# Where the first rows of x, the row moments and the diagonal sums are computed in a four-layer graph kernel, and in which order its second layer is entered

## The chip, the cores and the metric

The kernel runs on one core of a Trainium2 chip. The core has five engines with a queue each: TensorE (PE in the profile, its weight loads PEld), VectorE (DVE), ScalarE (ACT), GpSimd (POOL) and SyncE (SP), which here only issues DMA transfers. The engines run beside each other and wait for each other through semaphores; each queue is worked off in its order. The metric is the time of one execution on the device in microseconds (us), the median of several runs. Less is better.

## What is computed

Four graph layers over N = 2708 nodes with D = 128 features. Each has the form x = x + layer(relu(layernorm(x)), adj), with adj a 2708 x 2708 f32 matrix that is sparse but stored dense, and whose diagonal isn't zero. The reference, cut to the two layers that matter here:

```python
# layer 0
h = maximum(layernorm(x), 0)
msg = adj.T @ h
inv_deg = 1 / adj.sum(axis=0)             # 0 where infinite
x = x + msg * inv_deg[:, None]

# layer 1
h = maximum(layernorm(x), 0)
s = h @ msg_w[:, :D].T ;  d = h @ msg_w[:, D:].T
messages = gelu(s[:, None, :] + d[None, :, :] + msg_b)
agg = einsum('ijd,ij->id', messages, adj)
new = gelu(concat([h, agg]) @ upd_w.T + upd_b) + h
x = x + layernorm(new) * ln_w + ln_b
# layer 2: adj @ h and a GRU cell;  layer 3: two attention heads masked by adj
```

The kernel doesn't form all pairs in layer 1. For every row and every block of 124 columns, VectorE looks up the (at most 8) largest entries and their columns; this is done in layer 0, while adj passes through the memory on the chip. Layer 1 then works on those lists, with the diagonal taken apart.

## The kernel before

Rows go in tiles of 128 (22 tiles, NT), columns in blocks of 124 (22 blocks, NB). GROUPS are groups of four tiles (the last has two). At the start all of x is asked for on ScalarE's queue, and all 22 tiles are normalised ahead of layer 0. Cuts are marked (...).

```python
for t, k in GROUPS[:-1]:
    nc.scalar.dma_start(xs[:, t : t + k, :], x[t * P : (t + k) * P, :].rearrange("(t p) d -> p t d", p=P))
...                                            # two more loads for the last two tiles

def moments(src, name, pool=small):            # VectorE, and one power on GpSimd
    for q in range(k):
        nc.vector.bn_stats(st[:, q, :], src[q])
        nc.vector.bn_aggr(mv[:, q, :], st[:, q, :])
    nc.vector.tensor_scalar(r[:, 3, :], mv[:, :, 1], EPS, None, ALU.add)
    nc.gpsimd.tensor_tensor(r[:, 0, :], r[:, 3, :], minus_half[:, 0:k], ALU.pow)
    return mv, r
def factors(mv, r): ...                        # five small VectorE operations on [128, k]
def scale_rows(dst, src, rstd, shift, func):   # ScalarE, one activation a tile
    for q in range(len(src)):
        nc.scalar.activation(dst[q], src[q], func, bias=shift[:, q : q + 1], scale=rstd[:, q : q + 1])

for t, k in GROUPS:
    normalise(h, xs, t, k, AF.Relu, "n0")      # moments, factors, scale_rows
```

Layer 0. The tile rows of a group share one buffer `a4`, of which there are two. After the group, its 22 column tiles are turned on TensorE, and ScalarE takes them out with their sums and sends them to HBM for layers 2 and 3:

```python
for gi, (g0, gk) in enumerate(GROUPS):
    a4 = rows.tile([P, 4, N], F32, name="a")
    for q in range(gk):
        n = g0 + q
        a = a4[:, q, :]
        nc.sync.dma_start(a[0:m, :], adj[n * P : n * P + m, :])
        for ci, (c, cw) in enumerate(CHUNKS):  # six chunks of columns
            nc.tensor.matmul(accs[ci][:, 0:cw], h[0:m, n, :], a[0:m, c : c + cw], ...)
        nc.gpsimd.tensor_copy(near[:, 0 : c1 - c0], a[:, c0:c1])          # the blocks of the diagonal
        nc.gpsimd.tensor_tensor(dg[:, 0:m], a[:, d0 : d0 + m], ident[:, 0:m], ALU.mult)
        nc.gpsimd.tensor_tensor(near[:, ...], a[:, d0 : d0 + m], offdiag[:, 0:m], ALU.mult)
        nc.vector.reduce_sum(own[:, n : n + 1], dg[:, 0:m], AX.X)         # the diagonal, by row
        for b in range(NB):
            ...                                                           # ab: block b of a, or of near
            nc.vector.max(val[:, n, b, :], ab)
            nc.vector.max_index(col[:, n, b, :], val[:, n, b, :], ab)
        nc.scalar.activation(sign, a, AF.Sign, accum_out=total[:, n : n + 1])
    for j in range(NT):
        ...                                                               # transposes of the group
        nc.scalar.activation(aT[0:k, 0:iw], p[0:k, 0:iw], AF.Copy, accum_out=sums[0:k, j, gi : gi + 1])
        nc.sync.dma_start(adjT[0:k, j, i0 : i0 + iw], aT[0:k, 0:iw])
```

Layer 1 runs in periods, one for each tile t, and is pipelined over four tiles. A period works in six steps k; steps of later tiles are laid between the products of the present one:

```python
def period(t, between=()):
    now, c, b, a = (0 <= t + q < NT for q in range(4))
    last = 0 <= t - 1 < NT
    if c and not between:
        put_values(t + 1)                      # GpSimd, 8 operations
    for k in range(GB):
        for step in between[k : k + 1]:
            step()
        if now:
            combine(t, k)                      # TensorE, 24 products
            activate(t, k)
        if k < 2:
            if last: gather(t - 1, GB - 2 + k)
            if k == 0 and c: pass_on(t + 1)    # two DMAs, out to HBM and back, to all partitions
            if k == 1 and a: rank(t + 3)
            if k == 1 and last: close_tile(t - 1)
        elif now:
            gather(t, k - 2)
        if k in (1, 2) and b: fetch(t + 2, k - 1)
        if k == 1 and a: describe(t + 3)
        if k == 2:
            if now and t % 2 == 0 and t + 2 < NT: sources(t // 2 + 1)
            if a: select_rows(t + 3)           # VectorE: sel; then two DMAs: later = sel, one partition on
            if now and t + 4 < NT: count_rows(t + 4)
            updates(t)
        if k > 0 and c: put_more(t + 1, k)     # ScalarE, 14 in all
        if k == 3 and c: columns(t + 1)        # VectorE, on what pass_on brought
        if k == 3 and b: place(t + 2)          # VectorE, seven operations
        if k == 4 and a: finish_rows(t + 3)    # VectorE: sel -= later
```

Before the first period comes the prologue. For each group g of rows it adds layer 0's result to x (`enter`: scaled additions and moments on VectorE), scales (`rows`: factors on VectorE, scaling on ScalarE), turns (`turn_rows`: TensorE and ScalarE) and makes the columns' part of the messages (`destinations`: TensorE; its split into three bf16 parts goes ScalarE, VectorE, ScalarE, GpSimd). It also brings the first three tiles through rank, describe, select, finish, fetch and place. The kernel writes it as one list, in the order in which every engine gets its instructions:

```python
for step, n in (
    (spread_sums, 0), (count_rows, 0), (spread_sums, 1), (rank, 0), (enter, 0),
    (select_rows, 0), (describe, 0), (enter, 1), (spread_sums, 2), (rows, 0), (turn_rows, 0),
    (count_rows, 1), (rows, 1), (count_rows, 2), (count_rows, 3), (destinations, 0), (turn_rows, 1),
    (finish_rows, 0), (fetch_both, 0), (rank, 1), (enter, 2), ...
    (split_destinations, 3), (put_values, 0), (destinations, 4), (put_rest, 0), (finish_rows, 2),
):
    step(n)
period(0, (fourth, fifth))     # fourth, fifth: split of group 4, all of group 5, put_values(1)
for t in range(1, NT + 1):
    period(t)
```

Outside of such lists (`tc.manual_schedule`) the order of instructions on an engine is chosen when the kernel is built, so it isn't always that of the text.

Of the kernel before, what the change touches and what calls it, by code (L numbers as in the profile page):

```python
# [30 lines left out]
P = 128  # L31
N = 2708
# [28 lines left out]
def listed_layers(ctx: ExitStack, tc: tile.TileContext, x, adj, w, out, flag):  # L61
# [17 lines left out]
    for t, k in GROUPS[:-1]:  # L79
        nc.scalar.dma_start(xs[:, t : t + k, :], x[t * P : (t + k) * P, :].rearrange("(t p) d -> p t d", p=P))  # L80
    nc.scalar.dma_start(xs[:, FULL - 1, :], x[(FULL - 1) * P : FULL * P, :])
    nc.scalar.dma_start(xs[0:TAIL, FULL, :], x[FULL * P : N, :])
# [4 lines left out]
    def load(pool, name, shape=None):  # L87
        t = pool.tile(list(shape or w[name].shape), F32, name=name)
        nc.scalar.dma_start(t, w[name])
        return t  # L90

    def load_columns(pool, name):

        k = w[name].shape[0] // P
        t = pool.tile([P, k], F32, name=name)
        nc.scalar.dma_start(t, w[name].rearrange("(k p) -> p k", p=P), allow_slow_non_contiguous=True)
        return t

    def load_rows(pool, name):

        t = pool.tile([P, w[name].shape[0]], F32, name=name)
        nc.scalar.dma_start(t, w[name].partition_broadcast(P))
        return t


    minus_half = const.tile([P, 8], F32, name="minus_half")
# [50 lines left out]
    for t, k in GROUPS:  # L157
        normalise(h, xs, t, k, AF.Relu, "n0")
# [10 lines left out]
    HB = NB // 2  # L169
    HP = 8  # L170
    R = 4
    C = 4 * S + R + 1

    count = keep.tile([P, P], F32, name="count")
    nc.gpsimd.iota(count, [[1, P]], base=0, channel_multiplier=0, allow_small_or_imprecise_dtypes=True)
    count_h = keep.tile([P, P], BF16, name="count_h")
    nc.vector.tensor_copy(count_h, count)
    ident_h = keep.tile([P, P], BF16, name="ident_h")
    nc.vector.tensor_copy(ident_h, ident)
    part = keep.tile([P, 1], F32, name="part")  # L180
    nc.gpsimd.iota(part, [[0, 1]], base=0, channel_multiplier=1, allow_small_or_imprecise_dtypes=True)
    before = keep.tile([P, P], BF16, name="before")
    nc.vector.tensor_scalar(before, count, part, None, ALU.is_gt)
    ends4 = keep.tile([P, NB, R], BF16, name="ends4")
    rows_n = keep.tile([P, NT, NB], BF16, name="rows_n")
    ends = keep.tile([P, NT, NB], BF16, name="ends")
    later = keep.tile([P, NB, E], BF16, name="later")
    nc.gpsimd.memset(later, 0.0)
    xb = [keep.tile([P, NB, C], BF16, name=f"xb{q}") for q in range(2)]
    for q in range(2):  # L190
        nc.vector.tensor_copy(xb[q][:, :, 4 * S : 4 * S + R], part.unsqueeze(1).to_broadcast([P, NB, R]))

# [4 lines left out]
    with tc.tile_pool(name="l0c", bufs=1) as fix:  # L197
# [3 lines left out]
        nc.gpsimd.memset(sums, 1.0)  # L201
        with (
# [6 lines left out]
            for gi, (g0, gk) in enumerate(GROUPS):  # L209
# [4 lines left out]
                for q in range(gk):  # L214
# [3 lines left out]
                    nc.sync.dma_start(a[0:m, :], adj[n * P : n * P + m, :])  # L218
                    for ci, (c, cw) in enumerate(CHUNKS):
# [15 lines left out]
                    nc.vector.reduce_sum(own[:, n : n + 1], dg[:, 0:m], AX.X)  # L235
                    for b in range(NB):
# [4 lines left out]
                        nc.vector.max_index(col[:, n, b, :], val[:, n, b, :], ab)  # L241
                    sign = pool.tile([P, N], BF16, name="sign")
                    nc.scalar.activation(sign, a, AF.Sign, accum_out=total[:, n : n + 1])
                for j in range(NT):
# [31 lines left out]
    nc.vector.tensor_tensor(gate_b, b_ih[:, 0:2], b_hh[:, 0:2], ALU.add)  # L276
    nc.vector.tensor_scalar(gate_b, gate_b, 0.5, None, ALU.mult)
    half_b = late.tile([P, 1], F32, name="half_b")
    nc.vector.tensor_scalar(half_b, b_hh[:, 2:3], 0.5, None, ALU.mult)
# [6 lines left out]
    def layer3_weights():  # L286
# [13 lines left out]

    with (
# [18 lines left out]

        d3 = fix.tile([P, NB, 3, D], BF16, name="d3")
        def split(dst, src, rest):
# [273 lines left out]
        def period(t, between=()):  # L596
# [3 lines left out]
            if c and not between:  # L600
                put_values(t + 1)
            for k in range(GB):
                for step in between[k : k + 1]:
                    step()
# [36 lines left out]
        def spread_sums(g):  # L641
# [6 lines left out]
            state["p", g] = p  # L648

        def enter(g):  # L650

            t, k = GROUPS[g]
            p = state.pop(("p", g))
# [8 lines left out]
        def rows(g):  # L662
# [8 lines left out]
        def blocks_of(g):  # L671

            return 4 * g, min(4, NB - 4 * g)

        def destinations(g):

            b0, bn = blocks_of(g)
            p = bank("p_d")
            pv = p.rearrange("p (b d) -> p b d", b=4)
            for b in range(b0, b0 + bn):  # L680
                k = width(b)
                nc.tensor.matmul(pv[0:k, b - b0, :], hT[:, b * JB : b * JB + k], msg_wT[:, 1, :], start=True, stop=True)
            whole = bn if width(b0 + bn - 1) == JB else bn - 1
            state["d", g] = [
                (pv[0:k, q0:q1, :], [d3[0:k, b0 + q0 : b0 + q1, q, :] for q in range(3)], q0, q1, k)
                for q0, q1, k in ((0, whole, JB), (whole, bn, width(NB - 1)))
# [870 lines left out]
```

## Time and profile before

| what | value |
|---|---|
| time, median of 3 runs | 1110.0 us (1109.5 to 1110.35) |
| span of the profiled execution | 1108.1 us |
| TensorE busy, weight loads | 963.6 us (87%), 760.1 us (69%) |
| VectorE busy | 839.4 us (76%) |
| ScalarE busy | 504.2 us (46%) |
| GpSimd busy | 394.1 us (36%) |
| HBM read, written | 77.30 MB, 30.84 MB |
| mean granted clock of TensorE | 0.933 |

Busy times are sums over the whole span; the layers have different limits, so a stretch of the time has to be looked at by itself. A line of the timeline gives the start in us, the time of the instructions in us, the engine, the source line, the operation, what it writes and reads, how many were merged into the line, and in brackets how long the engine was idle before and what ended that. Times of instructions on one engine may overlap: a MAX8 lasts 0.28 us, and the next instruction starts 0.19 us after it. The source lines that matter: L116 to L119 are the moments, L125 to L129 the factors, L135 the scaling, L220 the products of layer 0, L235 the diagonal's sum, L240 and L241 the search, L243 the signs, L249 and L253 the transposes and their way out, L339 builds sel (and mine), L364 and L365 send later, L370 is finish_rows, L453 columns, L499 and L503 the products of layer 1.

### The profile page before, as it was taken

What the parts mean: (1) busy time and instruction counts of PE and PEld (TensorE: products, weight loads), DVE (VectorE), ACT (ScalarE), POOL (GpSimd) and SP (SyncE); (2) the same over time, 40 slices, a digit from 0 to 9 for tenths busy, and PEclk for the clock granted to TensorE, in tenths of its full rate; (3) what the DMA queues carried; (4) which work ended last, traced back from release to release, by engine and by line L of the source; (5) the groups of instructions that cost most, each with busy time, mean ns of one, the idle gap of its engine ahead of it and who ended that gap; (6) DMA issues with size and microseconds to landing.
All of it is one profiled execution on the core that took longest, in us unless ns stands there. A gap on an engine that the chain in (4) does not pass through costs nothing. (4 is left out here: it accounts for less than half of the span.)

```text
span 1108.1 us, 21904 instructions
## 1 busy us (share of the span) xinstructions
PE 963.6 (87%) x7968; PEld 760.1 (69%) x7968; DVE 839.4 (76%) x2948; ACT 504.2 (46%) x1319; POOL 394.1 (36%) x466
## 2 busy tenths in 40 slices
PE   3998887944389999999999979999979999999993
PEld 1455444523389999999898934444468899999772
DVE  5999999997766668676887255655578977997673
ACT  3857556623476666656676521433322200230142
POOL 4111111103385655776566253344310200340132
PEclk9999889755699999999999989999989999999996
DMA  9488978522133222322222056545300000000000
GB/s 361 164 299 281 324 259 288 178 64 68 46 106 102 96 86 90 106 86 101 83 103 80 28 193 209 190 157 198 100 18 1 1 9 1 1 20 1 2 15 14
DMA packets 55298, 125.39 MB, mean 113 GB/s; under 512 B 7414, under 2 KB 19782, under 8 KB 52472
## 3 DMA queue, kind: packets, MB, share of 16 engines
q1 hardware_dynamic: 48590, 121.12, 31.6%
q10 hardware_dynamic: 6590, 2.77, 1.0%
q8 instruction: 64, 1.05, 0.4%
q14 instruction: 54, 0.44, 0.1%
HBM read 77.30 MB, written 30.84 MB: 98 GB/s over the span
## 5 line engine op out<-in xcount | busy, mean ns | idle before, releaser
L838 PE MATMUL att<-hv,wt 128*128 128x129 f32 (+2 forms) x1936 | 240.7, 281 | 9.2 <-DVE wt L806 9.2
L838 PEld LDWEIGHTS att<-hv,wt 128*128 128x128 f32 (+2 forms) x1936 | 221.8, 190 | 26.2 <-DVE wt L806 9.1
L806 DVE SCALAR_TENSOR_TENSOR wt<-row,lift,mask 128x1024 f32<-128x1024 f32 (+5 forms) x176 | 160.0, 939 | 34.2 <-PE att L838 34.2
L423 POOL TENSOR_SCALAR put<-mine,value 128x128 f32<-128x128 bf16 x176 | 147.7, 855 | 72.4 <-DVE mine L339 70.0
L499 PE MATMUL p_m<-s,sel 128*128 128x128 bf16 x1452 | 160.8, 219 | 5.4 <-ACT g L511 5.4
L119 POOL TENSOR_TENSOR n_r<-n_r,minus_half 128x4 f32<-128x4 f32 (+1 forms) x36 | 51.3, 1425 | 316.1 <-DVE n_r L118 305.2
L503 PE MATMUL p_m<-d,cols 124*128 124x128 bf16 (+1 forms) x1452 | 161.0, 219 | 1.4 <-DVE cols L453 1.3
L220 PE MATMUL acc<-a,hs 128*128 128x512 f32 (+2 forms) x264 | 122.3, 599 | 27.6 <-DMA a<-in_adj 18.9
L524 PE MATMUL agg<-put,g 128*128 128x128 f32 (+1 forms) x968 | 135.8, 281 | 0.0
L241 DVE FIND_INDEX8 col<-val,a 128x8 uint16<-128x124 f32 (+1 forms) x441 | 118.6, 280 | 0.0
L959 PE MATMUL p_agg<-a,hs 128*128 128x512 f32 (+2 forms) x264 | 111.5, 564 | 7.7 <-DVE u L572 4.8
L524 PEld LDWEIGHTS agg<-put,g 128*128 128x128 f32 x968 | 118.1, 192 | 0.0
L499 PEld LDWEIGHTS <-sel 128*128 128x128 bf16 x1452 | 103.7, 97 | 10.8 <-issue 7.1
L503 PEld LDWEIGHTS <-cols 124*128 124x128 bf16 (+1 forms) x1452 | 101.8, 97 | 1.9 <-DVE cols L453 1.9
L240 DVE MAX8 val<-a 128x8 f32<-128x124 f32 (+1 forms) x441 | 102.6, 272 | 0.0
L511 ACT ACTIVATE g<-p_m 128x512 f32<-128x512 f32 x132 | 73.0, 553 | 63.6 <-PE p_m L503 63.6
L431 ACT ACTIVATE put<-mine,value 128x128 f32<-128x128 bf16 x308 | 100.5, 390 | 0.0
L220 PEld LDWEIGHTS acc<-a,hs 128*128 128x128 f32 (+1 forms) x264 | 49.7, 209 | 72.2 <-issue 43.4
L249 PEld LDWEIGHTS p_T<-ident,a 128*128 128x128 f32 x484 | 59.0, 146 | 52.8 <-ACT aT L253 25.4
L249 PE MATMUL p_T<-ident,a 128*128 128x128 f32 x484 | 77.7, 293 | 18.3 <-DMA a<-in_adj 10.0
L253 ACT ACTIVATE aT<-p_T 128x512 f32<-128x512 f32 (+2 forms) x132 | 70.9, 541 | 40.0 <-issue 16.3
L959 PEld LDWEIGHTS p_agg<-a,hs 128*128 128x128 f32 (+1 forms) x264 | 48.6, 196 | 56.6 <-issue 55.1
(228 smaller groups left out, 1396.6 us busy)
## 6 DMA issues: line engine op xcount, KB each, us to landing
a<-in_adj SPq DMA_DIRECT2D x21, 1354.0 KB
adjT<-aT SPq DMA_DIRECT2D x105, 256.0 KB
a<-adjT SPq DMA_DIRECT2D x20, 1280.0 KB
spread<-passed SPq DMA_DIRECT2D x22, 704.0 KB
later<-sel SPq DMA_DIRECT2D x22, 616.0 KB
later<-sel SPq DMA_DIRECT2D x22, 82.5 KB
adjT<-aT SPq DMA_DIRECT2D x21, 74.0 KB
a<-adjT SPq DMA_DIRECT2D x4, 370.0 KB
```

Of the source, the lines that this page charges most:

```text
L220: nc.tensor.matmul(accs[ci][:, 0:cw], h[0:m, n, :], a[0:m, c : c + cw], start=(n == 0), stop=(n == NT - 1))
L240: nc.vector.max(val[:, n, b, :], ab)
L241: nc.vector.max_index(col[:, n, b, :], val[:, n, b, :], ab)
L249: nc.tensor.transpose(p[0:k, q * P : q * P + m], a4[0:m, q, j * P : j * P + k], ident[0:m, 0:m])
L423: nc.gpsimd.tensor_scalar(st["put", 0][:, b, :], st["mine"][:, b, :], st["value"][:, b : b + 1], None, ALU.mult)
L431: nc.scalar.activation(st["put", 1][:, b - HP, :], st["mine"][:, b, :], AF.Identity, scale=st["value"][:, b : b + 1])
L499: nc.tensor.matmul(p[:, b - b0, :], st["sel"][:, b, :], s3[:, q, t % 2, :], start=(q == 0), stop=False)
L503: nc.tensor.matmul(p[:, b - b0, :], st["cols"][0:kb, b, :], d3[0:kb, b, q, :], start=False, stop=(q == 2))
L524: nc.tensor.matmul(agg, g[:, b - 4 * k, :], put, start=(b == 0), stop=False)
L806: nc.vector.scalar_tensor_tensor(wt[0:kj, :], row[0:kj, k, c : c + n], lift[0:kj, j, k : k + 1], mask[0:kj, j, c : c + n], op0=ALU.max, op ...
L838: nc.tensor.matmul(banks[s // 3][0:m, s % 3, :], wt[0:kj, q * P : q * P + m], hv[0:kj, j, k, :], start=(v < 2 and s // 3 not in touched), ...
L959: nc.tensor.matmul(pa[:, 0:n], h[0:k, j, :], a[0:k, j - j0, 0:n], start=(j == 0), stop=(j == NT - 1))
```

## The change

Two things at once.

Layer 0. The first four tiles of x are loaded ahead of adj on SyncE's queue, and only they are normalised ahead of layer 0; the rest of x follows behind the second tile row of adj. The moments of the other 18 tiles come from ScalarE, as sums and sums of squares of accumulating activations, with GpSimd for the small arithmetic; these are written behind the search of tile 2. The diagonal's sum goes from VectorE to ScalarE. Weights are loaded from SyncE's queue in place of ScalarE's. The purpose is to start the search earlier and to take work from VectorE in layer 0.

Prologue. The written list gives way to a loop over the groups, with periods -3, -2 and -1 put between; period 0 is like any other. The constants of layer 1 (count, part, before, later, xb) move from ahead of layer 0 into layer 1.

```diff
-    for t, k in GROUPS[:-1]:
-        nc.scalar.dma_start(xs[:, t : t + k, :], x[t * P : (t + k) * P, :].rearrange("(t p) d -> p t d", p=P))
-    ...
+    nc.sync.dma_start(xs[:, 0:4, :], x[0 : 4 * P, :].rearrange("(t p) d -> p t d", p=P))
+    def load_rest(): ...                    # the other rows, on nc.sync
 ...                                         # load, load_columns, load_rows: nc.scalar -> nc.sync
-    for t, k in GROUPS:
-        normalise(h, xs, t, k, AF.Relu, "n0")
+    normalise(h, xs, 0, 4, AF.Relu, "n0")
 ...                                         # count, part, before, later, xb: from here to layer 1
+        def moments_apart(pool):
+            for t in range(4, NT):
+                junk = pool.tile([P, D], F32, name="junk")
+                nc.scalar.activation(junk, xs[:, t, :], AF.Copy, accum_out=shifts[:, t - 4 : t - 3])
+            nc.gpsimd.tensor_scalar(shifts, shifts, -1.0 / D, None, ALU.mult)
+            for t in range(4, NT):
+                junk = pool.tile([P, D], F32, name="junk")
+                nc.scalar.activation(
+                    junk, xs[:, t, :], AF.Square, bias=shifts[:, t - 4 : t - 3], accum_out=ve[:, t - 4 : t - 3]
+                )
+            nc.gpsimd.tensor_scalar(ve, ve, 1.0 / D, EPS, ALU.mult, ALU.add)
+            nc.gpsimd.tensor_tensor(rstd, ve, minus_half[:, 0:RT], ALU.pow)
+            ...                              # five more of [128, 18] on nc.gpsimd
+            scale_rows(tiles_of(h, 4, RT), tiles_of(xs, 4, RT), rstd, shifts, AF.Relu)
                     nc.sync.dma_start(a[0:m, :], adj[n * P : n * P + m, :])
+                    if n == 1:
+                        load_rest()
-                    nc.vector.reduce_sum(own[:, n : n + 1], dg[:, 0:m], AX.X)
 ...                                         # the search
+                    if n == 2:
+                        moments_apart(pool)
                     nc.scalar.activation(sign, a, AF.Sign, accum_out=total[:, n : n + 1])
+                    nc.scalar.activation(dg[:, 0:m], dg[:, 0:m], AF.Copy, accum_out=own[:, n : n + 1])
 ...                                         # gate_b, half_b: computed in late_weights (layer 2)
-        def period(t, between=()):
+        def period(t):
-            if c and not between:
+            if c:
                 put_values(t + 1)
 ...
-            for step, n in ( ... the list ... ):
-                step(n)
-            period(0, (fourth, fifth))
-            for t in range(1, NT + 1):
+            for t in range(4):
+                count_rows(t)
+            steps = (enter, rows_and_turn, turn_rows, destinations)
+            fill = {0: -3, 2: -2, 4: -1}
+            for g in range(len(GROUPS) + len(steps) - 1):
+                for k in reversed(range(len(steps))):
+                    if 0 <= g - k < len(GROUPS):
+                        steps[k](g - k)
+                if g in fill:
+                    period(fill[g])
+            sources(0)
+            for t in range(NT + 1):
                 period(t)
```

In the new prologue `enter` holds spread_sums, `rows_and_turn` is the old rows, and `destinations` does its split at once.

## The prediction

> **What bounds the kernel now.** I read the 40 slices of the page first, then the busy times in stretches that I cut where the work changes, then the timeline at the three seams.
>
> The slices show who is full when; one slice is 27.7 us.
>
> ```profile
> PE   3998887944389999999999979999979999999993
> DVE  5999999997766668676887255655578977997673
> PEclk9999889755699999999999989999989999999996
> ```
>
> VectorE (DVE) is full from slice 2 to 9. Then TensorE and its clock sink for two or three slices, and after that TensorE is full to the end. So there are three regimes, and the change touches the first two. The stretches put times to them:
>
> ```profile
> core 0: us, PE busy (x) PEld busy (x) DVE busy (x) ACT busy (x) POOL busy (x), PEclk, DMA share, GB/s
> 0.00:21.40 21.40, 2.74 (x6) 1.42 (x7) 10.52 (x72) 5.77 (x8) 7.71 (x16) 1.00 0.97 341
> 21.40:244.20 222.80, 184.77 (x751) 106.89 (x750) 220.77 (x1493) 139.73 (x331) 31.56 (x67) 0.88 0.69 242
> 244.20:304.10 59.90, 23.79 (x133) 18.20 (x133) 47.28 (x159) 22.92 (x54) 16.71 (x20) 0.59 0.17 57
> 304.10:320.70 16.60, 13.64 (x194) 12.95 (x193) 9.14 (x17) 13.11 (x44) 15.87 (x22) 0.98 0.24 80
> 320.70:621.00 300.30, 291.34 (x4080) 281.27 (x4078) 220.23 (x422) 195.44 (x569) 190.34 (x239) 1.00 0.28 94
> ```
>
> In layer 0 (21.4 to 244.2) VectorE has 220.77 of 222.80 us, ScalarE 139.73, GpSimd 31.56. In the prologue of layer 1 (244.2 to 304.1) no engine is full; VectorE has the most, 47.28 of 59.90, so that stretch is a chain of waits. From 320.7 on the cycle is TensorE's.
>
> The seam at the start, from the timeline:
>
> ```profile
> 7.18 0.66 PE L249 MATMUL p_T<-ident,a 128*128 128x128 f32 x2 [7.18 <-DMA a<-in_adj]
> 11.05 0.49 DVE L116 BATCH_NORM_STATS2 n_st<-xs 128x6 f32<-128x128 f32 x2 [10.04 <-DMA xs<-in_x]
> 12.72 3.23 POOL L119 TENSOR_TENSOR n_r<-n_r,minus_half 128x4 f32<-128x4 f32 x3 [11.26 <-DVE n_r L118]
> 21.38 0.28 DVE L240 MAX8 val<-a 128x8 f32<-128x124 f32 x1
> ```
>
> The first row of adj is there at 7.18, yet VectorE waits for x until 11.05, does moments, and starts the search (MAX8) only at 21.38. The seam to layer 1:
>
> ```profile
> 233.68 0.19 ACT L253 ACTIVATION_READ_ACCUMULATOR aT<-p_T 20x1 f32 x1
> 244.04 0.26 DVE L241 FIND_INDEX8 col<-val,near 128x8 uint16<-128x104 f32 x1
> 244.48 0.25 DVE L333 TENSOR_SCALAR some<-val 128x176 bf16<-128x176 f32 x1
> ```
>
> ScalarE ends layer 0 ten us ahead of VectorE. So a us taken from VectorE in layer 0 is a us of the kernel, up to about ten beyond what ScalarE also moves. Last, inside the prologue:
>
> ```profile
> 250.05 1.62 DVE L339 TENSOR_TENSOR sel<-count_h,ends 128x2816 bf16<-128x2816 bf16 x1
> 258.02 1.61 DVE L370 TENSOR_TENSOR sel<-sel,later 128x2816 bf16<-128x2816 bf16 x1
> ...
> 297.21 1.62 DVE L339 TENSOR_TENSOR sel<-count_h,ends 128x2816 bf16<-128x2816 bf16 x1
> ...
> 303.51 2.51 DVE L370 TENSOR_TENSOR sel<-sel,later 128x2816 bf16<-128x2816 bf16 x1 [0.98 <-DMA later<-sel]
> ```
>
> The pair sel, then sel minus its shifted copy, has a DMA in between. For the first tile the list puts 6 us of other work there and VectorE doesn't wait. For the third it waits: 298.75 (when the next instruction follows sel) to 303.51, so the copy needs 4.8 us.
>
> **What the Trainium skill says.** "Perfetto Trace Analysis", Optimizing Scalar/DVE Operations: where VectorE is saturated, moving work to ScalarE or GpSimd may pay. The trace has just that case, 220.77 of 222.80. "ScalarE: Activation LUTs", What ACT_TABLE_LOAD costs: 186 ns plus 0.833 ns an element, 93 ns for each per-partition pointer, 93 ns of overlap. For 128 elements and two pointers that is 0.386 us; the trace has 12 scalings in 4.73 us, 0.394 each. So an estimate from that page for an accumulating activation without pointer is 0.20 us, plus the accumulator read, whose slot in the trace is 0.09 us (185 ns long, half of it overlapped). "DMA: Bandwidth & Descriptors", Issuing engines are not separate DMA queues: issuing from another engine saves only issue time. Moving the weight loads should therefore do nothing by itself; the trace has 0.33 to 0.7 us of ScalarE queue time for each, where ScalarE is idle.
>
> **Part one, layer 0.** (a) Start. The first 256 KB of x go ahead on SyncE's queue, then adj. At the 341 GB/s of the first stretch x takes 0.8 us and a row of adj (1354 KB) 4 us; with some 2.5 us of latency (first row at 7.18 before, beside other traffic) x lands near 4 and adj near 7.5. VectorE then has four moments only (8 instructions, 1.5 us), GpSimd one power of 1.0 us, and near needs three GpSimd operations (0.39, 0.46, 0.45) after adj lands. First search: about 9.0 instead of 21.4. (b) Moments of 18 rows leave VectorE; part of them ran after 21.4 too and disappears in the next number. (c) The diagonal's sum leaves: 45.39 to 45.58, 0.19 us a tile. Between the sum of tile 2 at 45.39 and the end at 244.2 lie 20 tiles: 9.94 us each. New: 9.75, and 22 of them are 214.5. End of the search: 9.0 + 214.5 + 1 for a stall = about 225, **19 us earlier**.
>
> (d) Does ScalarE keep up? It gets 36 accumulating activations, about 0.35 us with the bias pointer on half of them (13 us), 22 sums of a diagonal (0.3 to 0.4, 8 us), on top of 140: about 161 of 215. Early it is tight: x's rest lands near 16, copies to 23, squares to 31, GpSimd's eight small operations with a power 18 wide (from 0.69 for two and 1.01 for four columns, 0.16 a column, about 3.3) to 36, scaling to 44. Then signs, and 22 evictions that took 22 us before (45 to 67), give back the first adj buffer near 76; tile 8 lands near 81, and VectorE asks for it at 9 + 8 x 9.75 = 87. That holds with 6 us to spare. near for tile 3 sits behind GpSimd's moments, ready near 37, wanted near 41. At the end ScalarE and TensorE finished 49 us after the last group's first load at 185.5; VectorE frees that buffer at 9 + 16 x 9.75 = 165, so they end near 215, still ahead of 225.
>
> **Part two, the prologue.** The written list goes; groups are walked in order, with periods -3, -2 and -1 between, and VectorE keeps program order. I walk it with the durations above, zero being the end of the search. Constants that now sit here (0.76 us at 20.49 to 21.25, and src_self), degree (1.3), four counts (0.53 each): 4.9. enter(0) 2.8, rank, describe, select: 9.85. finish_rows(0) follows at once, so the copy's 4.8 us are naked: 16.2 with its 1.55. Factors(0) 1.0, enter(1): 20.0. Factors(1) follow enter(1) directly and wait for the power and its signals, 1.8: 22.8. enter(2), select(1), place(0) 4.0, finish_rows(1) with 0.8 of wait: 34.3. Split, factors, enter(3), split, factors with 0.4 of wait, enter(4): 43.7. select(2) 46.1; columns(0) wait for the spread copy (issued near 44.4 and 4.0 long as at 617.0 to 621.0) and end at 49.3; place(1), finish_rows(2): 54.9. The rest for groups 2 to 5 on VectorE: 60.7. Then comes a bare chain: scale 0.9, turn 2, destinations(4) and (5) 5, sources(0) 4. The first product of period 0 is at about 70, against 59.9 before: **10 us later**. Before, though, period 0 held the last two groups and took 16.6 (304.06 to 320.68); the period of the same kind after it took 14.85, and the first one skips a gather, so 14.3. That gives 2 back: **8 us lost**.
>
> Layers 1 to 3 after that are the same instructions; three tiny operations move to late_weights, under 0.5 us, beside TensorE. Sum: 1110 - 19 + 8 = **1099**.
>
> **Rivals.** (1) *ScalarE becomes the bound of layer 0.* For it: moments serialize on it before any evictions, and TensorE can't use tile 4 before 36. Against: 140 of 223 us busy now, ten us of slack at the end. If each accumulating activation took 0.6 instead of 0.35, buffers would come 9 us later and VectorE would wait 5 to 10 us: 1104 to 1110. (2) *The list was worth more than I count.* For it: VectorE was 79% busy under the list, and in-order waits propagate to all engines. If every period there waited its whole 4.8 us, and each of six factors 1.8, the loss is 15 or more: 1106. (3) *The list was worth nothing:* its 12.6 us of VectorE idle time are also mostly waits; if the new order hides its waits as well, only the gain is left: about 1090. (4) *Early start hidden:* if the scheduler orders the search behind near of tile 0 or x arrives behind adj, the start is near 13 and the result 1103.
>
> **Range and chances.** The start is known to 2 us, the pitch to 1% (2 us), a ScalarE stall costs 0 to 8, the prologue is known to 6 us. Together about 8: from 1089 to 1109. Two per cent is 22 us; faster than 1087.8 needs the whole gain and no loss. Chances: faster 0.10, same 0.87, slower 0.03.
>
> **What would show it.** The first MAX8 near 9 us; no DVE sum of the diagonal; end of FIND_INDEX8 near 225; VectorE still full from 10 on, with waits of GpSimd for ScalarE instead of for VectorE's sum. In the prologue: a wait of about 4.8 us of L370's successor on the copy of sel, waits on the power, and about 70 us from the last FIND_INDEX8 to the first product with cols. I'd be wrong if VectorE shows gaps on adj or near between 40 and 120, or if that distance stays at 60 or exceeds 80.

## The result, and the profile after

The changed kernel takes 1114.65 us (1113.64 to 1115.93), the kernel before 1110.17 in the runs beside it: ratio **1.0039**, 95% interval 1.0021 to 1.0056. It is slightly slower, 16 us above the predicted 1099 and outside the range.

First the same two rows of the 40 slices (27.8 us each), in the profile of the changed kernel:

```profile
PE   6889878843389999999999988999979999999993
DVE  7999999947656767687777364656568987997683
```

VectorE is busier in the first slice (7 instead of 5), as intended, but drops to 4 in slice 9, where it was full before. TensorE's hole is as long as it was. The stretches, cut at the changed kernel's own seams (search; from its end to the first instruction of layer 1; prologue; period 0), show where the time lies. The columns are those of the table shown for the kernel before.

```profile
8.10:223.90 215.80, 181.77 (x714) 102.98 (x714) 215.38 (x1458) 153.45 (x411) 33.73 (x75) 0.91 0.74 266
223.90:237.50 13.60, 11.81 (x38) 6.56 (x38) 0.00 (x0) 7.40 (x40) 0.00 (x0) 0.53 0.36 103
237.50:310.80 73.30, 23.78 (x140) 19.15 (x141) 51.77 (x163) 27.11 (x72) 26.82 (x35) 0.57 0.15 49
310.80:326.30 15.50, 15.50 (x189) 14.80 (x188) 6.06 (x12) 9.53 (x28) 7.07 (x12) 0.80 0.23 82
```

The second row is new: 13.6 us in which VectorE, third busy figure, does nothing. The third row is the prologue, 73.3 us instead of 59.9.

The timeline at both ends of the search, lines of VectorE and ScalarE:

```profile
8.09 0.48 DVE L242 MAX8 val<-a 128x8 f32<-128x124 f32 x2 [2.84 <-DMA a<-in_adj]
...
223.61 0.25 DVE L243 FIND_INDEX8 col<-val,near 128x8 uint16<-128x104 f32 x1
237.52 0.28 ACT L258 ACTIVATE aT<-p_T 20x148 f32<-20x148 f32 x1
237.54 0.25 DVE L362 TENSOR_SCALAR some<-val 128x176 bf16<-128x176 f32 x1 [13.68 <-ACT aT L258]
```

The search starts at 8.09 instead of 21.38 and ends at 223.9 instead of 244.3. But the next instruction of VectorE waits 13.68 us until ScalarE has taken out the last turned tile, aT. In the kernel before, ScalarE was done ten us ahead. **Layer 0 has a second loop: load rows, products and transposes, evictions (ScalarE taking the turned tiles out), stores. It ended at 233.8 before and ends at 237.8 now, so it has become the bound.** Of 20 us gained by the search, 7 reach layer 1 (244.5 to 237.5), and the prologue takes 13 away.

Inside the prologue, the lines of the timeline that differ most:

```profile
239.63 2.44 POOL L345 MEMSET later<- 128x2816 bf16 x1
239.64 2.52 DVE L334 CAST count_h<-count 128x128 bf16<-128x128 f32 x1
...
254.06 1.63 DVE L399 TENSOR_TENSOR sel<-sel,later 128x2816 bf16<-128x2816 bf16 x1 [4.79 <-DMA later<-sel]
...
287.67 0.95 DVE L482 TENSOR_SCALAR cols<-spread,part 128x2816 bf16<-128x2816 bf16 x1 [2.61 <-DMA spread<-passed]
```

The predicted naked wait for the shifted copy (one with no other work laid into it) is there, 4.79 us, and the wait for the spread copy. The first two lines belong together: a cast that took 0.20 us in the kernel before lasts 2.52 us here, beside a GpSimd memset of 2.44 us.

### The profile page after: what moved, and what is told of

The parts are those of the page before. It is cut to its first block, busy times and chain, and to the rows that moved or that the text cites. A ratio compares the mean times of both kernels' runs of the same rounds, so it can differ in the third digit from the quotient of the medians.

```text
span 1111.8 us, 21946 instructions
## 1 busy us (share of the span) xinstructions
PE 971.8 (87%) x7968; PEld 765.7 (69%) x7968; DVE 827.2 (74%) x2860; ACT 521.6 (47%) x1435; POOL 392.5 (35%) x469
## 3 DMA queue, kind: packets, MB, share of 16 engines
q8 instruction: 64, 1.05, 0.4%
## 5 line engine op out<-in xcount | busy, mean ns | idle before, releaser
L452 POOL TENSOR_SCALAR put<-mine,value 128x128 f32<-128x128 bf16 x176 | 145.4, 842 | 74.2 <-DVE mine L368 71.8
L223 PE MATMUL acc<-a,hs 128*128 128x512 f32 (+2 forms) x264 | 125.5, 617 | 24.3 <-DMA a<-in_adj 19.6
L121 POOL TENSOR_TENSOR n_r<-n_r,minus_half 128x4 f32<-128x4 f32 (+1 forms) x31 | 43.6, 1406 | 286.1 <-DVE n_r L120 272.1
L258 ACT ACTIVATE aT<-p_T 128x512 f32<-128x512 f32 (+2 forms) x132 | 71.0, 543 | 34.9 <-issue 17.3
```

The source lines that it names most:

```text
L452: nc.gpsimd.tensor_scalar(st["put", 0][:, b, :], st["mine"][:, b, :], st["value"][:, b : b + 1], None, ALU.mult)
```

## The experiments

The traces gave this table (us; "first product" is TensorE's first product with cols, the start of period 0). Kernels marked list have the old prologue.

| kernel | search | last eviction starts | layer 1 starts | first product | ratio to before, 95% |
|---|---|---|---|---|---|
| before | 21.4 to 244.3 | 233.5 | 244.5 | 304.4 | 1 |
| changed | 8.1 to 223.9 | 237.5 | 237.5 | 310.8 | 1.0039 [1.0021, 1.0056] |
| e1, list | 7.4 to 223.9 | 239.4 | 239.4 | 299.2 | 0.9928 [0.9916, 0.9941] |
| e2 | 18.9 to 241.6 | 232.9 | 241.5 | 314.0 | 1.0078 [1.0065, 1.0091] |
| e3 | 9.3 to 225.1 | 237.0 | 237.0 | 310.5 | 1.0068 [1.0042, 1.0094] |
| e4 | 7.7 to 227.2 | 237.9 | 237.9 | 311.8 | 1.0035 [1.0023, 1.0048] |
| e8 | 8.2 to 224.0 | 234.7 | 234.8 | 308.4 | 1.0016 [1.0006, 1.0027] |
| e5 | 8.9 to 289.7 | 283.0 | 289.2 | 361.8 | 1.0486 [1.0472, 1.05] |
| e6, list | 10.5 to 291.1 | 283.6 | 290.6 | 349.3 | 1.0389 [1.0375, 1.0403] |
| e7, list | 22.1 to 313.3 | 278.8 | 312.8 | 371.6 | 1.0604 [1.059, 1.0619] |
| e9 | 8.5 to 230.0 | 235.9 | 236.1 | 309.9 | 1.0021 [1.0011, 1.0031] |
| e10, list | 10.4 to 231.1 | 236.5 | 236.7 | 296.7 | 0.9909 [0.9893, 0.9924] |
| e11, list | 21.8 to 244.7 | 236.8 | 244.7 | 305.3 | 0.9996 [0.9988, 1.0005] |
| e12 | 7.9 to 224.3 | 241.0 | 241.0 | 310.5 | 1.0019 [1.001, 1.0028] |
| e13 | 7.2 to 222.9 | 236.8 | 236.9 | 313.6 | 1.0042 [1.0025, 1.006] |
| e14 | 8.0 to 225.8 | 239.6 | 239.6 | 312.9 | 1.0052 [1.0035, 1.0069] |
| e15 | 7.2 to 223.0 | 239.2 | 239.2 | 308.2 | 0.9998 [0.9988, 1.0008] |
| e16, list | 10.5 to 246.9 | 254.0 | 254.1 | 314.3 | 1.0083 [1.0065, 1.0101] |
| e17 | 8.6 to 279.9 | 274.5 | 279.8 | 352.6 | 1.0398 [1.038, 1.0417] |
| e18, list | 10.5 to 279.2 | 273.1 | 279.1 | 339.2 | 1.0302 [1.0285, 1.0319] |

### The two parts of the change, each alone

e1 has the new loads, layer 0 and late weights, and keeps the list; e2 has the old loads and layer 0, and the new prologue.

```diff
# e1, against the kernel before: layer 0 and late weights as in the changed kernel
-    for t, k in GROUPS: normalise(h, xs, t, k, AF.Relu, "n0")
+    normalise(h, xs, 0, 4, AF.Relu, "n0")        # the rest by moments_apart
# e2, against the changed kernel: the reverse of these lines, and the old diagonal sum
```

> The new layer 0 alone, with the written list kept. In the changed kernel VectorE ends the search at 223.6 (20.6 us earlier than before), but the last accumulation out of the transposes ends at 237.9 and the prologue starts there, 6.7 us earlier than before. Theory (a second loop of loads, products, transposes and stores ends layer 0): 6 to 8 us below the kernel before, near 1103.5. Rival (the two parts disturb each other, and the list would give the whole search gain back): near 1090.

> The new prologue alone, with the old layer 0. Theory (the two parts add): the changed kernel is 4.5 above, layer 0 is worth -6.7, so the prologue costs 11 to 13: near 1122. Rival (the prologue is slow only because ScalarE and TensorE come late out of layer 0): near 1115.

Measured: e1 **1101.54 us**, e2 **1118.35 us**. By the ratios the new layer 0 alone is worth 8.0 us and not 19; the prologue alone costs 8.7. e1 has VectorE's wait too, so it comes from layer 0 and not from the prologue that follows:

```profile
239.37 0.25 DVE L362 TENSOR_SCALAR some<-val 128x176 bf16<-128x176 f32 x1 [15.42 <-ACT aT L282]
```

From the start of layer 1 to the first product, e1 needs 59.8 us, as the kernel before (59.9); e2 needs 72.5 and the changed kernel 73.3. That is the price of the list. The parts don't add up: -8.0 + 8.7 is +0.7, the whole is +4.3. Most of the difference is in the table: in e2 the search starts 2.5 and layer 1 3.0 us earlier than before, since the constants have left VectorE's start for the prologue, and that helps as long as the search is the bound. In the changed kernel it isn't. The rest is within the intervals.

### What the second loop does not wait for

e3 puts the late weights back on ScalarE's queue, e4 the diagonal's sum on VectorE. e8 lets GpSimd issue the loads of adj from tile 8 on.

```diff
# e3, in load, load_columns, load_rows
-        nc.sync.dma_start(t, w[name])
+        nc.scalar.dma_start(t, w[name])
# e4
-                    nc.scalar.activation(dg[:, 0:m], dg[:, 0:m], AF.Copy, accum_out=own[:, n : n + 1])
+                    nc.vector.reduce_sum(own[:, n : n + 1], dg[:, 0:m], AX.X)     # ahead of the search of the tile
# e8
-                    nc.sync.dma_start(a[0:m, :], adj[n * P : n * P + m, :])
+                    (nc.sync if n < 8 else nc.gpsimd).dma_start(a[0:m, :], adj[n * P : n * P + m, :])
```

> The changed kernel, but weights (not x) loaded from ScalarE's queue again. Theory of the SyncE queue: eleven weight loads sit between the first stores (45.9 to 54.9 us) and move the whole second loop by the 3.7 us by which the load of tile 8 comes later (71.15 against 67.46): near 1111. Rival (they sit in gaps where SyncE waits for ScalarE anyway, as the prediction said): 1114 to 1115.

> The changed kernel, but the diagonal's sum back on VectorE. Rival (ScalarE's added work made the second loop late): 22 x 0.39 = 8.6 us less on ScalarE, near 1107 to 1109. Theory (the second loop waits for buffers and loads, not for ScalarE's work): the search ends 4 us later, near 228, still ahead of 237, and the time stays at 1113 to 1115.

> The changed kernel, with the rows of adj from tile 8 on loaded from GpSimd's queue, so that no load stands behind stores in SyncE's order. If the loads' place behind the stores paces the second loop, it ends 7 to 13 us earlier: 1101 to 1108. If the release of the buffer by the interleaved transposes paces it: within 2 us of 1114.65.

Measured: e3 1115.38 us, e4 1114.28, e8 1111.82. The queue of the weights is not the cause, nor are the 22 sums on ScalarE (0.31 us each): e3 is if anything slower, and in e3 and e4 the last eviction is within 0.5 us of the changed kernel's. e8 brings it 2.8 us forward; its time falls between its two forecasts, and its interval overlaps with the changed kernel's, so no gain is shown. More telling is what ScalarE waits for from 44 us on. Columns: what waits, for what, us in total, times, longest. First the changed kernel:

```profile
ACT sign L247 <- DMA a<-in_adj: 29.2, 10, 4.8
ACT aT L258 <- issue: 17.3, 10, 3.3
ACT aT L258 <- DMA adjT<-aT: 4.9, 7, 1.3
```

Then e8:

```profile
ACT aT L258 <- DMA adjT<-aT: 33.4, 16, 5.2
ACT sign L247 <- DMA a<-in_adj: 1.6, 2, 1.2
```

ScalarE runs in order. In the changed kernel the sign pass of a row stands between two evictions and waits for its row, 29 us in all, with the evictions behind it. With the loads on a queue of their own the rows are there, and ScalarE waits as long for the stores that should give an eviction buffer back: 34 us of waiting for transfers in one, 35 in the other. The kernel before has the same (28.8 and 5.8), hidden behind the search. Transfers aren't all of it: for the 17.3 us under "issue" the trace names no releaser, but TensorE works through each of these ten waits, in nine of them on the products of a row and then on the next turns.

### Layer 0 in written order

In e5 to e7 the instructions of layer 0 stand in the order in which they are written: loads two groups ahead, the transposes of a group after its products. e5 is the changed kernel so, e6 is e1, e7 the kernel before.

```diff
+            with tc.manual_schedule():
             for gi, (g0, gk) in enumerate(GROUPS):
-                ... the rows' loads, row by row, between the other work
+                ... fetch_rows(gi + 2) after the stores of the group
```

> The changed kernel, with layer 0 in written order: two groups of rows are loaded ahead, a group's 88 transposes follow its own products without products of the next group between, and the loads of the group after next stand behind them. Theory (the second loop is slow because of the order, not the work): evictions end well ahead of the search, the prologue starts at 224 in place of 237.5, and the time falls by 13 to 14, near 1101. Rival (TensorE or ScalarE simply has that much work): 1112 to 1116.

> The new layer 0 in written order, with the old list: theory 1101.5 less the 15.7 us by which evictions end after the search in the new layer 0 with the list (239.4 against 223.7): near 1086, better than both kernels. Rival: near 1101.

> Control: the kernel before, with only the order of layer 0 written as in the two runs above. Theory: in the kernel before the search ends layer 0 (244.0 against 233.5), so a faster second loop is worth nothing: 1108.5 to 1111. Rival (the second loop also slows the search): below 1105.

Measured: 1164.43, 1152.98 and 1177.28 us. All three missed, for a reason of their own: the search became slower, in e5 280.7 us for 22 tiles, 12.8 a tile instead of 9.8. As written, each block's index search follows its own maximum directly, and then a block takes 0.58 us (12.8 / 22) and not 0.44, with no wait in the trace; from the start of a maximum to that of the next instruction it is 0.30 us and not 0.19. (The text of e9 below takes 13.3 a tile and 0.16 us a block from the copies of near; by the search itself it is 12.8 and 0.14.) The scheduler had put two maxima ahead of two index searches. In e9 to e11 the program is written so; the diagonal has its own buffers, and its sums come after the evictions.

```diff
-    max(b); max_index(b)                                   # block by block
+    max(b); max(b + 1); max_index(b); max_index(b + 1)
```

> As e5_ordered_layer0, with the search written in pairs (two maxima, then their two indices, the order that the build chose by itself in the kernels before and after) and the diagonal's sums on ScalarE behind a group's evictions. In e5 the near copies are 13.3 us apart, 0.606 us a block, with no wait on VectorE: theory (an index right behind its own maximum costs VectorE 0.16 us more) says the search is back at 0.443 us a block, ends at 224, and the time is 1114.65 - 13.5 = 1101. Rival (the slow search of e5 comes from the shared work of the other engines in that order): the search stays above 12 us a tile and the time above 1140.

> The new layer 0 ordered and in pairs, with the old list: theory 1101.5 less 15 (evictions at 239.4 no longer end after the search at 223.7): near 1086. If the second loop is limited by data moved rather than by order: 1095 to 1102.

> Control: the kernel before, with layer 0 ordered and in pairs. The search ends it in both, so theory says 1108 to 1111. A time below 1105 would say that the second loop already cost time in the kernel before.

Measured: 1112.88, **1100.49** and 1109.82 us. The search has its pace back. In e9 it ends at 230.0 and not at 224, as VectorE waits 6.3 us for near: the zeroing of the last group's unused row stands ahead of it in GpSimd's written order and waits for the buffer. But the last eviction comes at 235.9 to 236.8, wherever the search starts: at 8.5, 10.4 or 21.8 us. In e11 the early start is absent and the loop still ends there, so in this order it isn't VectorE that holds it. e10 has the lowest median of the study; e1's interval overlaps with its own. ScalarE's waits in e9, from 44 us on, are those for TensorE (33.2 us, 23 times) and for stores (13.3); rows are there in time. In this order the products of a group (48 matmuls, 18.3 us) and its transposes and evictions (about 19) follow one another, and their sum is the pace.

### Is it TensorE's work?

e13 is the changed kernel without the products of ten of the 22 tiles. It leaves out those tiles' part of the message sums; all else is done.

```diff
-                    for ci, (c, cw) in enumerate(CHUNKS):
+                    for ci, (c, cw) in enumerate(CHUNKS if n % 2 == 0 or n == NT - 1 else []):
                         nc.tensor.matmul(...)
```

> The changed kernel without the layer-0 products of ten of its 22 tiles (the odd ones but for the last), so the summed messages lack those tiles; loads, search, transposes, evictions and stores are untouched. Theory now: TensorE's own work, about 18.3 us of products and 19 us of transposes for each group of four, sets the pace of the loop behind the search, 37 to 40 us a group, so it cannot end before 236. With half of the products gone a group costs about 28 us: evictions end by 226, the prologue of layer 1 starts at 224 to 227 instead of 237.5, total 1101 to 1104. Rival, buffers and loads: the loop is held by the order in which the adj buffers come back, not by TensorE's work; the evictions still end at 234 to 238, total 1111 to 1115.

Measured: 1114.18 us, the last eviction at 236.8 instead of 237.5. From 44 to 237 us TensorE's busy time falls from 164.6 to 138.4 us, and the loop ends as before. The rival's forecast came true, but the run doesn't clear TensorE, since two other things moved. TensorE's granted clock in that stretch was 0.80 instead of 0.88. And ScalarE got a new wait, while those under "issue" fell to 8.8 us:

```profile
ACT dg L248 <- POOL dg L234: 10.8, 3, 5.2
```

These three waits are for the diagonal sums that the change gave to ScalarE. GpSimd makes dg behind near, and near has two buffers that VectorE's search gives back:

```profile
182.89 0.39 POOL L232 COPY near<-a 128x248 f32<-128x248 f32 x1 [9.16 <-DVE col L243]
```

So from 139.6 us on the loop of e13 ran into the search. In the one full group ahead of that, from 69.6 to 107.6 us, it took 38.0 us instead of 39.8 (ends of the last evictions). My theory at that point, that TensorE's work sets the whole pace, fails in that group; how much TensorE holds after it, this run can't say.

e14 and e16 give TensorE its rows earlier: eight tiles of x ahead, with moments on VectorE, so that ScalarE has 14 left. e16 is e10 with that.

```diff
+                        if n == 1: normalise(h, xs, 4, 4, AF.Relu, "n4")
-        RT = NT - 4
+        RT = NT - 8
```

> The changed kernel with eight tiles of x ahead and their moments on VectorE, so ScalarE and GpSimd do 14 tiles instead of 18 and TensorE has h of tiles 4 to 7 before 30 us instead of at 37.6. Theory of the late start: TensorE's loop starts later than it could; the first eviction at about 38 to 40 instead of 44 and the last at 231 to 234 instead of 237.5, total 1108 to 1111. Rival: the first eviction moves and the last does not, since the loop is paced elsewhere later on; total 1113 to 1116. The 2 to 3 us of moments on VectorE end the search near 226, which is not the bound.

> The fastest kernel so far (new layer 0 in written order with pairs of maxima ahead of pairs of indices, old prologue of layer 1) with eight tiles of x ahead. If the late start of TensorE counts, its last eviction at 230 to 233 instead of 236.5 and total 1095 to 1098; if not, 1099 to 1102.

Measured: 1115.34 and 1119.17 us. h of tiles 4 to 7 is scaled at 32.6 us instead of 37.1, but the first eviction is at 44.7 instead of 44.3, since the scaling of the other 14 tiles still stands ahead of it on ScalarE. So e14 didn't move what it was meant to move, and says little. In e16, where VectorE keeps the written order, the search waits 17.7 us for near and ends 16 us later than in e10.

### Order or traffic

e17 (changed kernel) and e18 (e10) lace the two halves of TensorE's work: after every fifth eviction of a group come the products and the sign pass of one row of the next.

```diff
                         nc.sync.dma_start(adjT[0:k, j, i0 : i0 + iw], aT[0:k, 0:iw])
+                        if gi + 1 < len(GROUPS) and j % 5 == 4 and j // 5 < GROUPS[gi + 1][1]:
+                            sum_rows(g0 + 4 + j // 5, a4s[gi + 1][:, j // 5, :])   # products and sign
```

> The changed kernel with layer 0 in written order and pairs as in e9, and the products and the sign pass of the next group placed between the transposes and evictions of this one (one row after every fifth eviction). Theory: the second loop is held by order, not by work. In e9 a group's products (18 us) and its evictions (19 us) follow one another on TensorE while ScalarE waits, and in the changed kernel ScalarE waits with evictions behind it for rows that are not loaded yet. Laced, a group costs what ScalarE does, 22 evictions of 0.87 and 4 signs of 2.6, about 30 to 33 us instead of 37 to 40: the last eviction at 222 to 229 instead of 236, the prologue starts at 225 to 230, total 1101 to 1106. Rival, the traffic: loads and stores share one path, 11 MB a group, and take 36 us or more whatever the order; the evictions then wait for their stores, the last one stays at 233 to 238, total 1110 to 1114.

> As e17, with the old prologue of layer 1 (list kept), that is e10 laced. Theory of order: the last eviction at 222 to 229 instead of 236.5, total 1088 to 1094. Rival, the traffic: 1098 to 1102.

Measured: 1155.43 and 1143.04 us, both expectations missed by far, beyond the rival's. SyncE's queue in e17 (start and length in us; x4 are the four rows of a group):

```profile
127.30 2.11 SPq L221 DMA_DIRECT2D a<-in_adj  x4
129.51 46.74 SPq L284 DMA_DIRECT2D adjT<-aT  x22
176.42 1.90 SPq L221 DMA_DIRECT2D a<-in_adj  x4
```

And ScalarE's timeline in e17 after the first of these:

```profile
129.92 0.59 ACT L281 ACTIVATE aT<-p_T 128x512 f32<-128x512 f32 x1
146.87 0.60 ACT L281 ACTIVATE aT<-p_T 128x512 f32<-128x512 f32 x1 [16.27 <-DMA adjT<-aT]
```

Four rows, 5.5 MB, are asked for at once at 127.3. Then ScalarE fills its four eviction buffers, and waits 16.27 us for the first store behind these loads. From the fetch at 127.3 to the end of the wait the DMA engines are busy 0.92 of the time and move 348 GB/s, 6.8 MB, most of it these rows. Only then do the evictions go on, some 30 us. A group costs loads plus evictions, one after the other: 49 us from one fetch to the next. The Trainium skill, "DMA: Bandwidth & Descriptors", Two DMAs through the same engine are not ordered, says that within one queue of one DMA engine descriptors start in order; the trace shows what that means for a store behind four loads. VectorE ends later still, at 279.9, behind the last eviction: it waits 18.9 us for rows and, in one piece, 37.1 us for near, which stands in GpSimd's order behind the zeroing of the last group's unused row, as in e9.

In e9 the same fetch lies ahead of the products, when there is nothing to store, and costs little; in e17 it lies ahead of evictions. In the changed kernel the scheduler alternates loads and stores, and the 34 us appear in small portions, 29 of them at the sign passes.

### The prologue

e12 moves the constants back ahead of layer 0. e15 moves the finish of tile 0, with the naked wait for its copy, behind the work of group 1.

```diff
# e12
-        count_h = fix.tile([P, P], BF16, name="count_h")   # and ident_h, before, later, xb: in the prologue
+    count_h = keep.tile([P, P], BF16, name="count_h")      # the same, ahead of layer 0
# e15
-                if k == 4 and a:
+                if k == 4 and a and t > -3:
                     finish_rows(t + 3)
...
+                if g == 1:
+                    finish_rows(0)
```

> The changed kernel with the constants of layer 1 made ahead of layer 0 again. In the changed prologue count_h and before are drawn out to 242.15 while GpSimd sets later to zero (2.44 us). Theory: this alone is 2.5 to 3 us of the prologue, near 1112, as the search they would delay isn't what ends layer 0. Rival (hidden under the load of msg_wT and the counts): within 1 us of 1114.65.

> The changed kernel with the finish of tile 0 (the subtraction of the shifted copy and what follows it) three steps later in the program, behind the work of group 1. If the waits of the prologue add up as they are written, the wait of 4.8 us for the copy of tile 0 goes and 3 to 4.8 us of the prologue's 73 with it: total 1110 to 1112. Rival: the prologue is a chain whose waits hand over to one another, so that the time taken away here comes back at the next copy or at the spread: prologue still 72 to 74, total 1114 to 1116.

Measured: e12 1112.35 us, e15 **1110.48**. e12 shortens the prologue by 3.8 us (69.5), and the last eviction came 3.5 us later, so that no gain stands out: its interval overlaps with the changed kernel's. e15 is 4 us faster than the changed kernel, the prologue 69.0 instead of 73.3. The wait for the first copy in its trace:

```profile
255.69 1.63 DVE L399 TENSOR_TENSOR sel<-sel,later 128x2816 bf16<-128x2816 bf16 x1 [0.62 <-DMA later<-sel]
```

From 4.79 to 0.62: the waits of the prologue add up as written, and order alone takes the largest of them away.

## Why the prediction was wrong

**Right:** (a) the start, 8.1 against 9.0. (b), (c) the pace and the end of the search, 223.9 against 225, so 20 us earlier against 19. The costs on ScalarE: moments of 0.29 and 0.39 us plus the slot of their read, the sum of a diagonal 0.31. GpSimd's power of 18 columns took 3.25 us against 3.3, and the scaling ended at 44.1 us against 44.

**Wrong: step (d).** "VectorE frees that buffer at 9 + 16 x 9.75 = 165, so they end near 215, still ahead of 225." The time that it adds to 165 held: from the last group's first load to the end of the loop are 47 us (48 before, where the prediction has 49). VectorE was done with the buffer at 165 too. But VectorE isn't what frees it. In the changed kernel, VectorE's end of tile 15, the last transposes from the buffer of tiles 12 to 15, their last eviction and the load into that buffer:

```profile
165.08 0.26 DVE L243 FIND_INDEX8 col<-val,a 128x8 uint16<-128x104 f32 x1
188.43 1.19 PE L254 MATMUL p_T<-ident,a 128*128 128x128 f32 x8
189.75 0.57 ACT L258 ACTIVATE aT<-p_T 20x512 f32<-20x512 f32 x1
190.90 0.34 SPq L219 DMA_DIRECT2D a<-in_adj  x1
```

Between VectorE's last touch and the load lie 26 us. What comes last are TensorE's turns of the group, done at 189.6; then the load has to let the store of the last eviction go first in SyncE's order, issued by 190.7. And the kernel before had shown it:

```profile
174.53 0.27 DVE L241 FIND_INDEX8 col<-val,a 128x8 uint16<-128x104 f32 x1
183.03 1.18 PE L249 MATMUL p_T<-ident,a 128*128 128x128 f32 x8
184.36 0.57 ACT L253 ACTIVATE aT<-p_T 20x512 f32<-20x512 f32 x1
185.52 0.33 SPq L218 DMA_DIRECT2D a<-in_adj  x1
```

There VectorE was done with the buffer at 174.8, TensorE at 184.2, and it was loaded at 185.5. I used the 185.5 without asking which reader had held it. The prediction even had the limit in hand, "up to about ten beyond what ScalarE also moves"; step (d) set it aside by letting the loop come forward with VectorE. Loads of a group's first row follow one another at 37 to 41 us in both kernels (67.5, 107.6, 145.1, 185.5 before; 71.2, 112.4, 150.0, 190.9 after), though the search runs 13 to 20 us earlier in one: a loop with a pace of its own, which happened to be near the search's 39.

The loop starts with the first eviction, at 44.3 us in both kernels, so the earlier search didn't bring it forward. That the two starts agree is chance. Before, five sign passes stand ahead of it on ScalarE; now it is the moved moments, a wait for GpSimd's part of them, and the scaling:

```profile
37.05 7.03 ACT L137 ACTIVATE hs<-xs,flat 128x128 f32<-128x128 f32 x18 [4.40 <-POOL flat L200]
```

The first group's evictions then end at 72.1 us instead of 68.2, with 24.7 us of ScalarE's work between instead of 19.2: one sign pass more, and diagonal sums. This is as much as the 4 us by which the loop ends later. That it is their cause isn't shown: in e4, without the sums, the first group ends at 70.2, and the last eviction comes no earlier.

What holds the pace behind that start stays open. By e3 and e4 it isn't the weights' queue or the added sums; by the loads above, not the search. e13 doesn't clear TensorE, and e11 speaks for the written order alone. What the waits of ScalarE show is a ring of two row buffers and four eviction buffers, through which 11 MB a group go in and out, with TensorE's products between: e8 moved the wait from rows to stores, e9 to TensorE, e17 back to stores, and with the new layer 0 the loop never ended before 234.7. One of the changed kernel's longest waits for a row, and the whole loop (the last two columns are the DMA engines' busy share and GB/s):

```profile
114.86:119.53 4.67, 0.69 (x5) 0.42 (x4) 4.67 (x34) 0.01 (x2) 0.00 (x0) 0.93 0.90 325
44.00:237.00 193.00, 164.58 (x688) 96.08 (x686) 179.82 (x1216) 128.97 (x341) 21.85 (x50) 0.88 0.71 249
```

In the four longest of these waits the share is 0.90 to 0.93: while ScalarE waits for a row, the DMA engines are nearly full, and over the loop they aren't. The Trainium skill, "Perfetto Trace Analysis", Optimization Strategy, says that a gap repeating over a stretch, on the engine that should be saturated, can mean too few buffers; ScalarE isn't saturated here, but its ten waits for rows repeat in that way. Whether more buffers would spread the traffic was not tried.

**The prologue** was right in kind and 3.3 us too short: 73.3 against 70. Counted as the prediction has it, from the last FIND_INDEX8 to the first product with cols, it is 86.9 us, since VectorE's wait comes on top; that is past the 80 which it gave as a sign of being wrong. Against the kernel before VectorE has 4.5 us more of work and 8.9 more of idle time. The walk had put the constants at 0.76 us; beside the memset, from 239.2 to 242.5, they took about 3. Period 0 gave back 1.1 us instead of 2.

Together: 12.5 (layer 1 starts at 237.5, not 225) + 3.3 + 0.9 = 16.7, against 15.65 us missed; the end of the kernel, behind the last attention product, was 1.8 us shorter in this trace than in that of before.

**The rivals.** That ScalarE becomes the bound came nearest: there is a wait of VectorE, and the moved work fills most of ScalarE's time up to the loop's start. But its reason, dearer activations, is not it: they cost what was estimated, and VectorE's wait comes behind the search, not for buffers within it. For the list's worth, e1 and the changed kernel are 12 us apart, and the prologue 13.5: between my 10 and the rival's 15.

## What to carry to other kernels

Before an engine that bounds a stage is relieved, find every loop that runs beside it and how far behind it ends: here ten us, so as long as that loop stays where it is, the gain cannot exceed ten. A buffer's release is read from its last reader in the trace, not from the busiest one. And where loads and stores share a queue and a few buffers, reordering can move the wait about and hardly shorten the loop, as in e8 and e9. A run that takes work from one engine shows what that engine held only if no new wait has come up elsewhere, as one did in e13.

## What the runs showed of the hardware

- An index search right behind the maximum it uses costs VectorE 0.14 us a block (e5: 0.58 against 0.44 in the changed kernel), without a wait in the trace; two maxima ahead of two searches avoid it (e9).
- A GpSimd memset of 128x2816 bf16, 2.44 us, holds up VectorE's casts beside it: 2.52 instead of 0.20 us; so in e2, e9 and e13 too. The Trainium skill, "SBUF — State Buffer", SBUF: two separate sides, describes a port pair that VectorE and GpSimd lock for a whole instruction; this case agrees.
- A store behind 5.5 MB of loads on the same queue waits for about all of them; ScalarE, with its four eviction buffers full, stands still for 16.3 us (e17).
